# Routed expert tiles: transposes between the two projections, TensorE in written order, gathers three tiles ahead

## The chip, the core and the metric

The kernel runs on one core of a Trainium2 chip. The core has five engines with a queue each: TensorE (PE in the profile; PEld is its weight load), VectorE (DVE), ScalarE (ACT), GpSimd (POOL) and SyncE (SP), and 16 DMA engines that move data between memory and the on-chip buffers. Instructions of one engine run in the order of its queue; engines wait for one another by semaphores. The metric is the device time of one execution in microseconds (us), and lower is better.

## What is computed

The reference is one decoder layer over 4 sequences of 512 tokens with 512 features, all in float32: a causal self-attention, a cross-attention against a context, and a feed-forward part, each behind a layer norm and added to its input. Only the last part matters here. Each token is sent to 2 of 8 experts; each expert is a gated network with 352 hidden units.

```python
topk_p, topk_i = jax.lax.top_k(probs, K)                 # K = 2 of E = 8 experts
comb = (jax.nn.one_hot(topk_i, E) * topk_p[..., None]).sum(axis=1)
h1 = jnp.einsum('nc,eic->eni', xf, w1)                   # 512 -> 352, for each expert
h2 = jnp.einsum('nc,eic->eni', xf, w2)
h = jax.nn.silu(h1) * h2
eo = jnp.einsum('eni,eci->enc', h, w3)                   # 352 -> 512
y = jnp.einsum('enc,ne->nc', eo, comb).reshape(Bq, Tq, Cq)
sh = jax.nn.silu(xf @ sw1.T) * (xf @ sw2.T) @ sw3.T      # shared expert, every token
return y + sh.reshape(Bq, Tq, Cq)
```

## The kernel before

The two attentions, the shared expert and the choice of experts fill the first 1729 us and are the same in both kernels. At their end `out` holds the result without the routed part, and `normed` (in memory) holds the normed tokens.

**Routing.** The kernel computes only what the router asks for. The 4096 pairs of a token and an expert are sorted by expert and cut into tiles of 128 rows, each of one expert, with padding: `NTILE` = 39 tiles. `picked[:, t]` holds the token numbers of tile t, `gain[:, t]` the weights, `owner[0, t]` the expert. Which expert a tile has is known only at run time, so PE reads it into a register (L1088, a TENSOR_LOAD in the profile) and addresses `w1all`, `w2all` and `w3all`, which hold the weights of all experts, by it. For the same reason a wait for these weights covers the loads of all experts.

**One tile, first half: `enter`.** `fetch` (L1050) gathers 128 rows into `xg` by an indirect DMA on POOL's queue (L1053; four buffers), PE turns them in four transposes (L171, by `transpose_in`) into a bank of PSUM, and ScalarE copies the bank to `xT` (L172). Then come PE's read of the owner, the projections h1 and h2 (L1102: for each four matmuls over 352 columns, which the profile shows as eight), the silu of h1 on ScalarE (L1110, `sl`), and the product `hm` on VectorE (L1112).

**Second half: `leave`.** PE turns `hm` in three transposes into `ht` (L1118; one bank), VectorE copies it to `hT` in two pieces (L1120, L1121), PE multiplies it with w3 into `y` (L1124; three matmuls over 512 columns, six in the profile; one bank), ScalarE scales it into `yo` (L1132; two buffers), and POOL issues an indirect DMA (L1134) that adds the rows to `out`. These scatter-adds all write `out`, so each waits for the one before.

**Order.** The loop (L1146) enters tile t and then leaves tile t - 4 (`BEHIND` = 4); four tiles are left after the loop. The program is written in that order, but the framework's scheduler decides the order of the instructions on each engine, except where `tc.keep_in_program_order` is called on an instruction. Here only the owner's read is held. In the steady part the scheduler makes it, on PE: h1, h2 of tile t; ht of tile t - 4; the transposes of the rows of tile t + 1; the owner of tile t + 1; y of tile t - 4. On VectorE it is hm, then the two hT copies; on POOL gathers and scatters alternate. The class `Ordered` (L356) wraps an engine so that its instructions are held in program order while `pinned` is true; `tensor` is PE wrapped so. The attention part uses it and sets `pinned` back to False at L896. The wrapper's line, L362, is then the line that the profile shows.

**Before the loop.** The first two tiles' rows are fetched among the last jobs of the shared expert (L1068). The loads of w3 (L1081, L1084) are on SP's queue and start when the shared expert's weights are no longer needed, at 1728.3 us. The loads of w1 and w2 (L1047, L1048) are issued before that, the last at 1681.0 us.

Of the kernel before, what the change touches and what calls it, by code (L numbers as in the profile page):

```python
# [8 lines left out]
F32 = mybir.dt.float32  # L9
BF16 = mybir.dt.bfloat16  # L10
AF = mybir.ActivationFunctionType
ALU = mybir.AluOpType
# [3 lines left out]
P = 128  # L16
B, S, HID = 4, 512, 512
NT = S // P
NC = HID // P
NKV, QPG, D = 4, 4, 128  # L20
XKV, XG, XD = 8, 4, 16
E, I = 8, 352
# [5 lines left out]
NTILE = (2 * B * S + E * (P - 1)) // P  # L28
# [7 lines left out]
def decoder_kernel(  # L36
# [15 lines left out]
    nc = tc.nc  # L52
# [5 lines left out]
    ident = const.tile([P, P], F32, tag="ident", name="ident")  # L58
# [108 lines left out]
    def transpose_in(ps, src, dst, s, copy, bufs=2):  # L167

        t = ps.tile([P, NC, P], F32, tag="t", name="t", bufs=bufs)
        for c in range(NC):  # L170
            nc.tensor.transpose(t[:, c, :], src[:, c * P : (c + 1) * P], ident)  # L171
        copy(dst[:, :, s * P : (s + 1) * P], t)  # L172
# [6 lines left out]
    with ExitStack() as ph:  # L179
        wp = ph.enter_context(tc.tile_pool(name="wattn", bufs=1))  # L180
        p2 = ph.enter_context(tc.tile_pool(name="a2", bufs=2))
        ps = ph.enter_context(tc.tile_pool(name="aps", bufs=2, space=PSUM))
# [7 lines left out]
        for g in range(NKV):  # L190
            t = wp.tile([P, NC, (QPG + 1) * D], F32, tag=f"wqk{g}", name=f"wqk{g}")
            nc.sync.dma_start(t, wqkv_v[:, :, g, : (QPG + 1) * D])
            wqk.append(t)
            t = pj.tile([P, QPG, HID], F32, tag=f"wpr{g}", name=f"wpr{g}")
# [37 lines left out]
        def project(b, g, h, xnT):  # L232

            pq = ps.tile([P, S], F32, tag="mm", name=f"pq{b}_{g}_{h}")
            for c in range(NC):
                nc.tensor.matmul(  # L236
                    pq,
                    lhsT=wqk[g][:, c, h * D : (h + 1) * D],
                    rhs=xnT[:, c, :],
                    start=c == 0,  # L240
                    stop=c == NC - 1,
                )
            if h == QPG:
                t = p2.tile([P, S], F32, tag="kT", name=f"kT{b}_{g}")
                nc.scalar.copy(t, pq)
            else:
                t = p2.tile([P, S], F32, tag="qT", name=f"qT{b}_{g}_{h}", bufs=3)
                nc.scalar.mul(t, pq, QSCALE)  # L248
            return t
# [71 lines left out]
        late = None  # L321
# [10 lines left out]
        for b in range(B):  # L332
            xnT, v = norm_and_v(b)
            for g in range(NKV):
                kT = project(b, g, QPG, xnT)
                outs = []
                for h in range(QPG):
# [4 lines left out]
                    late = (b, g, h, pr, v, outs)  # L342
# [11 lines left out]
    pinned = False  # L354

    class Ordered:  # L356
# [12 lines left out]
    tensor, vector, scalar, gpsimd, sync = (  # L369
        Ordered(e) for e in (nc.tensor, nc.vector, nc.scalar, nc.gpsimd, nc.sync)  # L370
    )
# [108 lines left out]
    with ExitStack() as ph:  # L480
# [45 lines left out]
        def enter(b):  # L526

            xn = p2.tile([P, NT, HID], F32, tag="xn", name=f"cxn{b}", bufs=1)
            parts = norm_parts(
                b, lambda s: xn[:, s, :], vector, gpsimd, vector if b == 0 else gpsimd  # L530
            )
            ctxT = p2.tile([P, S], F32, tag="ctxT", name=f"ctxT{b}", bufs=1)
            xnT = p2.tile([P, NC, S], F32, tag="xnT", name=f"cxnT{b}", bufs=1)
            ctxTs[b], xnTs[b] = ctxT, xnT

            def values():
                gpsimd.tensor_copy(
                    vpad[b % 2][:, :, :, 0:XD],
                    ctxs[b].rearrange("p s (k d) -> p s k d", d=XD),
                )  # L540

            def keys():
                t = single(f"tc{b}")
                for s in range(NT):
                    tensor.transpose(quarter(t, s), ctxs[b][:, s, :], ident)
                scalar.copy(ctxT, t)

            def tokens(s):
                t = single(f"tx{b}_{s}")
                for c in range(NC):  # L550
                    tensor.transpose(quarter(t, c), xn[:, s, c * P : (c + 1) * P], ident)
                scalar.copy(
                    xnT[:, :, s * P : (s + 1) * P],
                    t.rearrange("p (c d) -> p c d", c=NC),
                )

            return parts + [values], [keys] + [lambda s=s: tokens(s) for s in range(NT)]
# [245 lines left out]
        pinned = True  # L803
# [6 lines left out]
        for i in range(NU * 8 + LAG + 4):  # L810
# [35 lines left out]
            b, u = divmod(n, XKV)  # L846
# [57 lines left out]
    with ExitStack() as ph:  # L904
# [142 lines left out]
            nc.sync.dma_start(w1all[:, e], w1T[e].rearrange("(c p) i -> p c i", p=P))  # L1047
            nc.sync.dma_start(w2all[:, e], w2T[e].rearrange("(c p) i -> p c i", p=P))  # L1048

        def fetch(t, ps, bufs):  # L1050

            xg = rx.tile([P, HID], F32, tag="xg", name=f"xg{t}", bufs=4)
            nc.gpsimd.indirect_dma_start(  # L1053
                out=xg,
                out_offset=None,
                in_=normed,
                in_offset=bass.IndirectOffsetOnAxis(ap=picked[:, t : t + 1], axis=0),
            )
            xT = rx.tile([P, NC, P], F32, tag="xT", name=f"xT{t}")
            transpose_in(ps, xg, xT, 0, nc.scalar.copy, bufs)  # L1060
            return xT

        jobs = shared_jobs(
            B - 1, lambda name: ps.tile([P, S], F32, tag="fill", name=name, bufs=4)
        )
        for job in jobs[:-12]:
            job()
        fetched = [fetch(t, ps, 1) for t in range(2)]  # L1068
        for job in jobs[-12:]:
            job()  # L1070
    late_sh.close()
# [3 lines left out]
    with ExitStack() as ph:  # L1075
        wl = ph.enter_context(tc.tile_pool(name="wall3", bufs=1, side="right"))
        p2 = ph.enter_context(tc.tile_pool(name="r2", bufs=2))
        ps = ph.enter_context(tc.tile_pool(name="rps", bufs=2, space=PSUM))
        w3all = wl.tile([P, E, len(IC), HID], F32, tag="w3all", name="w3all")
        for e in range(E):  # L1080
            nc.sync.dma_start(  # L1081
                w3all[:, e, 0:2, :], w3T[e, 0:256].rearrange("(c p) d -> p c d", p=P)
            )
            nc.sync.dma_start(w3all[0 : I - 256, e, 2, :], w3T[e, 256:I])  # L1084

        def enter(t):
            xT = fetched[t] if t < len(fetched) else fetch(t, ps, 2)
            loads, (e,) = nc.values_load_multi_w_load_instructions(  # L1088
                owner[0:1, t : t + 1],
                engines=[mybir.EngineType.PE],  # L1090
                min_val=0,
                max_val=E - 1,
                skip_runtime_bounds_check_because="a count of at most E - 1 by its minimum",
                bass_reorder=False,
            )
            for i in loads:
                tc.keep_in_program_order(i)
            h1 = ps.tile([P, I], F32, tag="h1", name=f"h1_{t}")
            h2 = ps.tile([P, I], F32, tag="h2", name=f"h2_{t}")
            for h, w in ((h1, w1all), (h2, w2all)):  # L1100
                for c in range(NC):
                    nc.tensor.matmul(  # L1102
                        h,
                        lhsT=xT[:, c, :],
                        rhs=w[:, e, c, :],
                        start=c == 0,
                        stop=c == NC - 1,
                    )
            sl = p2.tile([P, I], F32, tag="sl", name=f"sl{t}")
            nc.scalar.activation(sl, h1, AF.Silu)  # L1110
            hm = p2.tile([P, I], F32, tag="hm", name=f"hm{t}", bufs=BEHIND + 2)
            nc.vector.tensor_tensor(hm, h2, sl, ALU.mult)  # L1112
            return t, e, hm

        def leave(t, e, hm):
            ht = ps.tile([P, len(IC), P], F32, tag="ht", name=f"ht{t}", bufs=1)
            for ic, (i0, m) in enumerate(IC):
                nc.tensor.transpose(ht[:m, ic, :], hm[:, i0 : i0 + m], ident)  # L1118
            hT = p2.tile([P, len(IC), P], F32, tag="hT", name=f"hT{t}")
            nc.vector.tensor_copy(hT[:, 0:2, :], ht[:, 0:2, :])  # L1120
            nc.vector.tensor_copy(hT[: I - 256, 2, :], ht[: I - 256, 2, :])  # L1121
            y = ps.tile([P, HID], F32, tag="y", name=f"y{t}", bufs=1)
            for ic, (_, m) in enumerate(IC):
                nc.tensor.matmul(  # L1124
                    y,
                    lhsT=hT[:m, ic, :],
                    rhs=w3all[:m, e, ic, :],
                    start=ic == 0,
                    stop=ic == len(IC) - 1,
                )  # L1130
            yo = p2.tile([P, HID], F32, tag="yo", name=f"yo{t}", bufs=2)
            nc.scalar.activation(yo, y, AF.Copy, scale=gain[:, t : t + 1])  # L1132

            nc.gpsimd.indirect_dma_start(  # L1134
                out=rows,
                out_offset=bass.IndirectOffsetOnAxis(ap=picked[:, t : t + 1], axis=0),
                in_=yo,
                in_offset=None,
                bounds_check=B * S - 1,
                oob_is_err=False,  # L1140
                compute_op=ALU.add,
            )

        BEHIND = 4
        late = []
        for t in range(NTILE):  # L1146
            late.append(enter(t))
            if len(late) > BEHIND:
                leave(*late.pop(0))
        for now in late:  # L1150
            leave(*now)


# [46 lines left out]
```

## Time and profile before

| | |
|---|---|
| median of 3 runs | 2084.8 us (2084.55 to 2087.17) |
| the profiled execution | 2085.54 us |
| its span, first to last instruction | 2083.8 us |
| TensorE clock granted, mean | 0.997 |
| PE busy over the span | 2029.6 us (97%) |
| VectorE, ScalarE, POOL busy over the span | 864.6, 679.5, 197.3 us |

The routed part in stages, from the profile's windows (us from the span's start; busy time of each engine):

| stage | length | PE | VectorE | ScalarE | POOL | DMA share |
|---|---|---|---|---|---|---|
| 1729.2 to 1757.9: tiles entered before the first is left | 28.7 | 26.91 | 3.02 | 5.75 | 3.04 | 0.82 |
| 1905.1 to 2043.7: the steady loop, 16 tiles of it | 138.6 | 133.04 | 16.78 | 27.77 | 38.03 | 0.28 |
| 2043.7 to 2070.2: the last y of the steady loop, and the tail | 26.5 | 23.26 | 3.55 | 4.22 | 6.20 | 0.24 |
| 2070.2 to 2083.8: after the last matmul | 13.6 | 0 | 0 | 0.69 | 3.10 | 0.01 |

A row of the timeline reads: start, length, engine, line, operation, output and input, how many; in square brackets the idle time of the engine just before it and what ended it. Matmuls are pipelined, so the length of one is longer than its share of PE: the distance from one start to the next is what it costs. "128x352" is partitions by elements. An entry that ends in q, like PEldq, is the engine's sequencer, which runs control instructions and does not count as busy.

### The profile page before, as it was taken

What the parts mean: (1) busy time and instruction counts of PE and PEld (TensorE: products, weight loads), DVE (VectorE), ACT (ScalarE), POOL (GpSimd) and SP (SyncE); (2) the same over time, 40 slices, a digit from 0 to 9 for tenths busy, and PEclk for the clock granted to TensorE, in tenths of its full rate; (3) what the DMA queues carried; (4) which work ended last, traced back from release to release, by engine and by line L of the source; (5) the groups of instructions that cost most, each with busy time, mean ns of one, the idle gap of its engine ahead of it and who ended that gap; (6) DMA issues with size and microseconds to landing.
All of it is one profiled execution on the core that took longest, in us unless ns stands there. A gap on an engine that the chain in (4) does not pass through costs nothing. (4 is left out here: it accounts for less than half of the span.)

```text
span 2083.8 us, 22685 instructions
## 1 busy us (share of the span) xinstructions
PE 2029.6 (97%) x8507; PEld 948.5 (46%) x8507; DVE 864.6 (41%) x1843; ACT 679.5 (33%) x1479; POOL 197.3 (9%) x182
## 2 busy tenths in 40 slices
PE   7999999999999999999999999999999999999996
PEld 4555555554555555542233333333333445555553
DVE  4433344442344334436666656566563351111111
ACT  2322332232223323323555454444444101111121
POOL 1000000000000000010202202020200011222222
PEclk9999999999999999999999999999999999999999
DMA  7000000000000000010003100100110255323321
GB/s 282 0 1 0 1 0 1 0 0 1 0 1 0 1 0 0 1 32 14 16 16 100 32 16 22 42 15 13 42 27 1 95 199 160 59 56 57 57 49 23
DMA packets 52509, 74.81 MB, mean 36 GB/s; under 512 B 9889, under 2 KB 27809, under 8 KB 52402
## 3 DMA queue, kind: packets, MB, share of 16 engines
q1 hardware_dynamic: 43666, 54.73, 8.5%
q0 software_dynamic: 8736, 18.62, 4.7%
q8 instruction: 70, 1.15, 0.2%
q14 instruction: 37, 0.30, 0.0%
HBM read 47.60 MB, written 18.61 MB: 32 GB/s over the span
## 5 line engine op out<-in xcount | busy, mean ns | idle before, releaser
L362 DVE TENSOR_REDUCE cnmx<-s 128x1 f32<-128x512 f32 x512 | 329.3, 685 | 199.3 <-PE s L362 199.2
L362 ACT ACTIVATE w<-s 128x512 f32<-128x512 f32 x512 | 277.9, 595 | 339.0 <-PE s L362 338.9
L362 PE MATMUL s<-ckT,cqT 32*128 32x512 f32 x1024 | 308.8, 640 | 1.0 <-DVE cnmx L362 1.0
L236 PE MATMUL pq<-xnT,wqk 128*128 128x512 f32 x640 | 300.9, 593 | 0.0
L362 PE MATMUL s<-cqT,ckT 32*128 32x512 f32 x1024 | 294.8, 640 | 0.0
L268 DVE TENSOR_REDUCE nmx<-sc 128x1 f32<-128x128 f32 (+3 forms) x256 | 125.8, 491 | 185.0 <-PE sc L265 184.8
L271 ACT ACTIVATE pr<-sc,nmx 128x128 f32<-128x128 f32 (+3 forms) x256 | 135.0, 527 | 156.0 <-DVE nmx L268 156.0
L294 DVE COPY prT<-tp 128x128 f32<-128x128 f32 (+2 forms) x192 | 97.0, 507 | 206.4 <-PE tp L290 206.3
L258 PE MATMUL sc<-kT,qT 128*128 128x128 f32 (+3 forms) x512 | 181.4, 463 | 0.0
L312 PE MATMUL pj<-wpr,oT 128*128 128x512 f32 x384 | 171.8, 596 | 0.0
L362 PE MATMUL sh<-fnT,sw 128*128 128x512 f32 x320 | 154.0, 613 | 0.0
L297 PE MATMUL po<-prT,v 128*128 128x512 f32 (+3 forms) x512 | 149.5, 434 | 4.3 <-DVE prT L294 4.3
L236 PEld LDWEIGHTS pq<-xnT,wqk 128*128 128x128 f32 x640 | 110.7, 191 | 85.5 <-issue 85.4
L362 PEld LDWEIGHTS s<-cqT,ckT 32*128 32x128 f32 x1024 | 80.7, 183 | 145.3 <-ACT w L362 108.6
L1112 DVE TENSOR_TENSOR hm<-h,sl 128x352 f32<-128x352 f32 x39 | 20.5, 525 | 284.6 <-PE h L1102 279.1
L362 PE MATMUL cpo<-w,vpad 128*32 128x512 f32 x1024 | 137.3, 608 | 0.0
L297 PEld LDWEIGHTS po<-prT,v 128*128 128x128 f32 x512 | 96.8, 190 | 84.3 <-issue 45.4
L1124 PE MATMUL y<-w3all,hT 128*128 (+1 forms) x234 | 109.8, 605 | 15.1 <-DVE hT L1120 15.1
L248 ACT ACTIVATE qT<-pq 128x512 f32<-128x512 f32 x64 | 38.2, 597 | 225.0 <-PE pq L236 225.0
L258 PEld LDWEIGHTS sc<-kT,qT 128*128 128x128 f32 x512 | 81.6, 189 | 56.1 <-ACT qT L248 20.2
L312 PEld LDWEIGHTS pj<-wpr,oT 128*128 128x128 f32 x384 | 69.5, 190 | 77.3 <-issue 71.0
L290 PE MATMUL tp<-ident,pr 128*128 128x128 f32 x640 | 102.3, 275 | 1.3 <-DVE prT L294 1.3
(162 smaller groups left out, 2000.6 us busy)
## 6 DMA issues: line engine op xcount, KB each, us to landing
w1all<-in_w1T SPq DMA_DIRECT2D x8, 704.0 KB
w2all<-in_w2T SPq DMA_DIRECT2D x8, 704.0 KB
wqk<-in_wqkvT SPq DMA_DIRECT2D x4, 1280.0 KB
x<-in_x SPq DMA_DIRECT2D x4, 1024.0 KB
wpr<-in_wprojT SPq DMA_DIRECT2D x4, 1024.0 KB
cqT<-cxnT SPq DMA_DIRECT2D x128, 32.0 KB
ckT<-ctxT SPq DMA_DIRECT2D x128, 32.0 KB
normed<-fxn SPq DMA_DIRECT2D x4, 1024.0 KB
```

Source lines behind the costliest of these rows:

```text
L236: nc.tensor.matmul(pq, lhsT=wqk[g][:, c, h * D : (h + 1) * D], rhs=xnT[:, c, :], start=c == 0, stop=c == NC - 1,)
L248: nc.scalar.mul(t, pq, QSCALE)
L258: nc.tensor.matmul(sc[:, :n], lhsT=qT[:, i * P : n], rhs=kT[:, :n], start=True, stop=False,)
L268: nc.vector.tensor_reduce(nmx[:, i : i + 1], sc[:, :n], AX.X, ALU.max, negate=True)
L271: nc.scalar.activation(pr[:, OFF[i] : OFF[i] + n], sc[:, :n], AF.Exp, bias=nmx[:, i : i + 1], accum_out=sm[:, i : i + 1],)
L290: nc.tensor.transpose(t[:, j, :], pr[:, OFF[i] + j * P : OFF[i] + (j + 1) * P], ident)
L294: copy(prT[:, : i + 1, i * P : (i + 1) * P], t[:, : i + 1, :])
L297: nc.tensor.matmul(po[:, j * P :], lhsT=v[j][:, g, :], rhs=prT[:, j, j * P :], start=j == 0, stop=j == NT - 1,)
L312: nc.tensor.matmul(pj, lhsT=outs[h][:, s * P : (s + 1) * P], rhs=wpr[g][:, h, :], start=h == 0, stop=h == QPG - 1,)
L362: i = getattr(self.engine, name)(*args, **kw)
L1112: nc.vector.tensor_tensor(hm, h2, sl, ALU.mult)
L1124: nc.tensor.matmul(y, lhsT=hT[:m, ic, :], rhs=w3all[:m, e, ic, :], start=ic == 0, stop=ic == len(IC) - 1,)
```

## The change

`fetch` is split: `gather_rows(t)` issues the gather, `turn_rows(t)` the four transposes and the copy to `xT`. Gathers of three tiles are issued before the loop, and each pass of the loop begins with that of tile t + 3; `xg` still has four buffers. `enter` and `leave` are split too. One pass of the loop is now, in this order: the gather of t + 3, the owner of tile t, h1 and its silu; the ht transposes and hT copies of the oldest waiting tile; the transposes of the rows of tile t + 1; h2 and hm; and last y, yo and the scatter of the waiting tile. All PE instructions of the loop go through `tensor` with `pinned` true, so this is their order on PE. How many tiles are left in a pass is `count`: none in tiles 0 to 3, one from tile 4 on, and two in tiles 12, 16 and 20, after which a tile is left one pass after it was entered, and one tile is left after the loop. The second of two does its ht transposes after h2. Banks and buffers keep their numbers. On PE the owner's read stands between y of one pass and h1 of the next; on VectorE the hT copies stand before hm. SP's queue keeps its order.

```diff
-        def fetch(t, ps, bufs):
-
+        xgs, xTs = {}, {}
+
+        def gather_rows(t):
             xg = rx.tile([P, HID], F32, tag="xg", name=f"xg{t}", bufs=4)
             nc.gpsimd.indirect_dma_start(
...
+            xgs[t] = xg
+
+        def turn_rows(t, ps, bufs=2):
+
             xT = rx.tile([P, NC, P], F32, tag="xT", name=f"xT{t}")
-            transpose_in(ps, xg, xT, 0, nc.scalar.copy, bufs)
-            return xT
+            bank = ps.tile([P, NC, P], F32, tag="t", name=f"xt{t}", bufs=bufs)
+            for c in range(NC):
+                tensor.transpose(bank[:, c, :], xgs[t][:, c * P : (c + 1) * P], ident)
+            nc.scalar.copy(xT, bank)
+            xTs[t] = xT
...
-        fetched = [fetch(t, ps, 1) for t in range(2)]
+        for t in range(3):
+            gather_rows(t)
+        for t in range(2):
+            turn_rows(t, ps, 1)
...
-        def enter(t):
-            xT = fetched[t] if t < len(fetched) else fetch(t, ps, 2)
+        def owner_of(t):
             loads, (e,) = nc.values_load_multi_w_load_instructions(
...
+            return e
+
+        def project(t, e, w, tag):
+            h = ps.tile([P, I], F32, tag=tag, name=f"{tag}_{t}")
+            for c in range(NC):
+                tensor.matmul(
+                    h,
+                    lhsT=xTs[t][:, c, :],
...
+            return h
+
+        def turn_hidden(t, hm):
             ht = ps.tile([P, len(IC), P], F32, tag="ht", name=f"ht{t}", bufs=1)
             for ic, (i0, m) in enumerate(IC):
-                nc.tensor.transpose(ht[:m, ic, :], hm[:, i0 : i0 + m], ident)
+                tensor.transpose(ht[:m, ic, :], hm[:, i0 : i0 + m], ident)
             hT = p2.tile([P, len(IC), P], F32, tag="hT", name=f"hT{t}")
             nc.vector.tensor_copy(hT[:, 0:2, :], ht[:, 0:2, :])
             nc.vector.tensor_copy(hT[: I - 256, 2, :], ht[: I - 256, 2, :])
+            return hT
+
+        def leave(t, e, hT):
...
         BEHIND = 4
+        pinned = True
         late = []
         for t in range(NTILE):
-            late.append(enter(t))
-            if len(late) > BEHIND:
-                leave(*late.pop(0))
-        for now in late:
-            leave(*now)
+            if t + 3 < NTILE:
+                gather_rows(t + 3)
+            e = owner_of(t)
+            h1 = project(t, e, w1all, "h1")
+            sl = p2.tile([P, I], F32, tag="sl", name=f"sl{t}")
+            nc.scalar.activation(sl, h1, AF.Silu)
+            count = 0 if t < BEHIND else 2 if len(late) > 1 and t % 4 == 0 and t > 8 else 1
+            now, late = late[:count], late[count:]
+            turned = [(u, o, turn_hidden(u, hm)) for u, o, hm in now[:1]]
+            if 1 < t + 1 < NTILE:
+                turn_rows(t + 1, ps)
+            h2 = project(t, e, w2all, "h2")
+            hm = p2.tile([P, I], F32, tag="hm", name=f"hm{t}", bufs=BEHIND + 2)
+            nc.vector.tensor_tensor(hm, h2, sl, ALU.mult)
+            late.append((t, e, hm))
+            turned += [(u, o, turn_hidden(u, hm)) for u, o, hm in now[1:]]
+            for some in turned:
+                leave(*some)
+        for u, o, hm in late:
+            leave(u, o, turn_hidden(u, hm))
+        pinned = False
```

More of the change, by code (lines that the diff above doesn't have):

```diff
@@ L1097, in enter @@
                 tc.keep_in_program_order(i)
[L1098 to L1115, printed above, removed]
+            return e
[5 more added lines that the diff above has]
+                    lhsT=xTs[t][:, c, :],
+                    rhs=w[:, e, c, :],
+                    start=c == 0,
+                    stop=c == NC - 1,
+                )
+            return h
+        def turn_hidden(t, hm):
             ht = ps.tile([P, len(IC), P], F32, tag="ht", name=f"ht{t}", bufs=1)
             for ic, (i0, m) in enumerate(IC):
-                nc.tensor.transpose(ht[:m, ic, :], hm[:, i0 : i0 + m], ident)
+                tensor.transpose(ht[:m, ic, :], hm[:, i0 : i0 + m], ident)
             hT = p2.tile([P, len(IC), P], F32, tag="hT", name=f"hT{t}")
@@ L1121, in leave @@
             nc.vector.tensor_copy(hT[: I - 256, 2, :], ht[: I - 256, 2, :])
+            return hT
+        def leave(t, e, hT):
             y = ps.tile([P, HID], F32, tag="y", name=f"y{t}", bufs=1)
             for ic, (_, m) in enumerate(IC):
-                nc.tensor.matmul(
+                tensor.matmul(
                     y,
@@ L1130, in leave @@
                 )
-            yo = p2.tile([P, HID], F32, tag="yo", name=f"yo{t}", bufs=2)
+            yo = p2.tile([P, HID], F32, tag="yo", name=f"yo{t}")
             nc.scalar.activation(yo, y, AF.Copy, scale=gain[:, t : t + 1])
```

## The prediction

> **What bounds the kernel now.** I read the page first (TensorE, PE in the rows, is busy 97% of the span), then the PE timeline of the routed tiles, where all of the diff lies, then the rows of all engines around one wait there, then the tail. PE's timeline, one tile of the steady part and the start of the next (start, length, operation, idle time before):
>
> ```profile
> 1847.17 2.53 PE L1102 MATMUL h<-w1all,xT 128*128 x8
> 1849.54 2.53 PE L1102 MATMUL h<-w2all,xT 128*128 x8
> 1851.91 0.49 PE L1118 MATMUL ht<-ident,hm 128*128 128x128 f32 x3
> 1852.24 0.60 PE L171 MATMUL t<-ident,xg 128*128 128x128 f32 x4
> 1853.18 2.82 PE L1124 MATMUL y<-w3all,hT 128*128 x6 [0.34 <-DVE hT L1120]
> 1855.83 2.53 PE L1102 MATMUL h<-w1all,xT 128*128 x8
> ```
>
> A tile takes 8.66 us (1847.17 to 1855.83). PE's own work is, start to start: both projections 2 x 2.37, three ht transposes 0.33, four t transposes 4 x 0.11 (three starts in 0.60 less one length of 0.27), y 6 x 0.43 = 2.57: 8.08. Lost are **0.58 us a tile**: 0.50 between the t transposes and y, and 0.08 because y's first weight load then stands open (2.65 from y to the next h instead of 2.57). The rows around the wait say why:
>
> ```profile
> 1912.52 0.49 PE L1118 MATMUL ht<-ident,hm 128*128 128x128 f32 x3
> ...
> 1912.79 0.53 DVE L1112 TENSOR_TENSOR hm<-h,sl 128x352 f32<-128x352 f32 x1 [7.61 <-PE h L1102]
> 1912.85 0.60 PE L171 MATMUL t<-ident,xg 128*128 128x128 f32 x4
> 1913.23 0.41 DVE L1120 COPY hT<-ht 128x256 f32<-128x256 f32 x1
> ...
> 1913.57 0.28 DVE L1121 COPY hT<-ht 96x128 f32<-96x128 f32 x1
> ...
> 1913.80 2.82 PE L1124 MATMUL y<-w3all,hT 128*128 x6 [0.35 <-DVE hT L1120]
> ```
>
> y needs hT, hT waits on VectorE behind hm, and hm could only start when h2 ended. Only 0.44 us of transposes cover that. Nothing else is near: in 1905.14:2043.70 the granted clock is 1.00 and the DMA share 0.28. The end of the kernel:
>
> ```profile
> 2063.61 2.82 PE L1124 MATMUL y<-w3all,hT 128*128 x6 [0.61 <-DVE hT L1120]
> ...
> 2066.99 1.55 POOL L1134 DMA_INDIRECT out<-yo,picked  x1 [3.88 <-issue]
> ...
> 2067.36 2.82 PE L1124 MATMUL y<-w3all,hT 128*128 x6 [0.61 <-DVE hT L1120]
> ...
> 2070.63 0.69 ACT L1132 ACTIVATE yo<-y,gain 128x512 f32<-128x512 f32 x1 [3.44 <-DMA out<-yo,picked]
> 2071.28 1.55 POOL L1134 DMA_INDIRECT out<-yo,picked  x1 [2.73 <-DMA out<-yo,picked]
> 2074.72 1.55 POOL L1134 DMA_INDIRECT out<-yo,picked  x1 [1.90 <-DMA out<-yo,picked]
> ```
>
> Four second halves are left after the loop. Each y comes 3.75 us after the last (2063.61 to 2067.36) against 2.90 of work, and the scatter-adds, which follow one another (starts 5.36, 5.42, 4.29 and 3.44 us apart), are by then the last to finish: from the last y to the end of the span 16.44 us.
>
> **The change, part by part.** Work on PE up to the start of the last y is the same in both: 78 projections x 2.37 + 37 sets of t x 0.44 (two stand before the loop) + 39 ht x 0.33 + 38 y x 2.57 = 311.8 us. Before, it took 2067.36 - 1729.21 = 338.2: 26.4 us lost, namely 34 tiles x 0.58 = 19.7; 1.0 at the y of tile 34; four tail leaves x 0.85 = 3.4; tiles 2 to 4, whose h1 waits for its own xT, 1.6; the rest is rounding.
>
> - *Both sets of transposes between h1 and h2.* The hT copies now run beside h2. In the tail, where no hm is in front of them, y can start 1.10 us after the first ht (2066.26 to 2067.36); in the change ht, t and h2 last 0.33 + 0.44 + 2.37 = 3.14: 2.0 us to spare. hm falls behind them on VectorE and is next needed a tile later. xT (0.58 on ScalarE) hides behind the same h2. So the 0.58 goes in all 35 steady leaves, and the 1.6 of tiles 2 to 4. What is late next is PE itself; ScalarE's order stays silu, xT, yo.
> - *A new border, transposes to a projection, 37 times.* The nearest row is before the loop, four t transposes and then a matmul of the shared part: 1717.61 to 1718.08, 0.47 against 0.44 of work, and 0.49 the time before. I take 0.04 each: 1.5 us. Bounds: 0, and one open weight load of 0.19 (mean of h's loads), 7 us.
> - *The read of the tile's owner* (L1088) stood between t and y, beside the wait; now it stands between y and h1, where no stall covers it:
>
> ```profile
> L1088 PEldq TENSOR_LOAD <-owner x39: 295/301/826, 1720.3 to 2039.2; - x39
> ```
>
>   Median 0.30 us. Behind it on PE's queue are h1 and all that follows. The last one ran at 2039.2, while the transposes it follows end at about 2043.3: the sequencer is 4 us ahead. In the change it is held at y's wait until hT is there, some 2 us before y can start, and y runs 2.57 more. Tile 1 already has the new order (h2, read, h1) and no gap: the next rows show h2 at 1731.65 and h1 at 1734.02, 2.37 apart. Here a rule speaks against the change: the Trainium skill ("DMA: Bandwidth & Descriptors", Latency and other measured facts) gives a tensor_load a floor of about 600 ns. Exposed in 35 tiles that is 21 us, an estimate, and nearly all of the gain; by the row 35 x 0.30 = 10.5. The row decides the size, tile 1 the cover: I take 0 and keep 10.5 as the bound.
>
> ```profile
> 1729.21 2.61 PE L1102 MATMUL h<-w1all,xT 128*128 x8 [0.94 <-issue]
> 1731.65 2.53 PE L1102 MATMUL h<-w2all,xT 128*128 x8
> 1734.02 2.53 PE L1102 MATMUL h<-w1all,xT 128*128 x8
> ```
>
> - *Gathers three tiles ahead:* nothing. There are four buffers as before; POOL already issues four gathers at 1689.6 to 1693.7 and the fifth at 1717.19 when tile 0 is transposed. One lands in 3.4 us (8.2 at worst), needed two tiles later. On POOL's queue a gather can stand behind a scatter; it has 16 us to spare. SP's list is unchanged.
> - *Two leaves in tiles 12, 16 and 20.* y has one bank, so the second waits for yo of the first: as in the tail 3.75 against 2.57, 1.18 each, 3.5 us. Their scatters go out 3.75 apart, and the next 8 us later: no queue builds up.
> - *w3.* Any y waits for all of w3, because the expert is a number known at run time. y of tile 0 comes at 1729.21 + 4.74 + 3 x 5.22 + 5.55 = 1755.2 instead of 1757.89. The DMA windows:
>
> ```profile
> 1752.00:1754.00 2.00, 2.00 (x7) 1.31 (x8) 0.00 (x0) 0.00 (x0) 0.36 (x1) 1.00 0.44 137
> 1754.00:1756.00 2.00, 2.00 (x8) 1.32 (x7) 0.00 (x0) 0.46 (x1) 0.00 (x0) 1.00 0.04 14
> ```
>
>   The load (last two numbers: DMA share, GB/s) ends by about 1754: I take 0, bound 1.5.
> - *The tail.* One leave is left; its y waits for hm, ht and yo as each tail y did: 0.85.
>
> Lost after: 1.5 + 3.5 + 0.85 = 5.9, so the last y starts at 1729.2 + 311.8 + 5.9 = 2046.9, 20.4 us earlier. From there: 2.90 to yo (1913.80 to 1916.70), 0.96 to the scatter, 9.08 from its start to the end (2074.72 to 2083.8), and 0.55 because the scatter before it was issued 3.75 ago and I take 4.3 between two (bounds 0 and 1.7): 13.5 instead of 16.4. Span 2060.4, **23.4 us less**. The profiled execution took 2085.54 (1.74 over its span): 2062.1. The median of the runs stands 0.74 lower: **2061.4**.
>
> **The rivals.**
> - *A rest of the stall stays at the new borders* (the owner's read exposed by its 0.30, or an open weight load at each): +7 to +10.5, 2068 to 2072. For it: y's wait still holds PE's sequencer once a tile. Against: 2 us of cover, and tile 1.
> - *The period stays at 8.66,* so that the change does not do what it says, because something other than hT ends the wait. Then the tail (3.4 - 0.85 + 2.9), less 3.5 for the double leaves, plus 1.6 at the start: 3.6 us less, 2081. Against: 0.16 us lies between the first hT copy's end (1913.64) and y, every tile.
> - *PE drains at the owner's read (slower).* Tile 0 shows the price: between the shared part's last matmul and h1 lie 0.94 us, put down to "issue", with the read waiting for semaphores. If y's wait leaves the queue empty in each of 35 tiles: 2061.4 + 32.9 = 2094. It decides from 23.4 / 35 = 0.67 us a tile. Against: tile 0's read waits for PE itself, the others do not.
>
> **How the numbers follow.** Forecast 0.78, rest of the stall 0.12, period unchanged 0.05, drain 0.05. Low end: no border cost, no scatter wait, and some 2 us for rows that I read as full: 2056. High end: the first rival's 2072. That leaves out the last two, 0.10, and a little. This kernel's measurement can tell 0.2%, 4.2 us, from no change: faster 0.90; the unchanged period, at 3.6, counts as the same: 0.05; slower 0.05.
>
> **What would show it.** In the changed kernel: a period near 8.1 us wherever one tile is left; no idle row before y except in tiles 12, 16, 20 and the last; h2 0.77 to 0.85 after the first ht; h1 2.57 after y's start; last y near 2047; 13 to 14 us from it to the end. A wait before h1 put down to "issue" would make the first or third rival right, an idle row before y the second, a DMA wait at tile 0's y the w3 term.

## The result and the profile after

The changed kernel takes **2060.86 us** (median of 4 runs, 2059.55 to 2061.09); the kernel before, run beside it, 2085.94 (4 runs, 2084.55 to 2087.17). The ratio is 0.9879, with a 95% interval of 0.9862 to 0.9896: some 25 us less. The profiled execution after took 2059.55 us, with a span of 2057.7 and a granted clock of 0.998. The first projection of tile 0 (h1) starts at 1729.31 us, against 1729.21 before, so all of the difference lies in the routed tiles.

TensorE's timeline after, a steady tile with the start of the next, and then the two adjacent y in the pass of tile 12 (columns as before; line 362 is the helper that now issues every TensorE instruction):

```profile
1757.71 2.53 PE L362 MATMUL h<-w1all,xT 128*128 x8
1760.08 0.49 PE L362 MATMUL ht<-ident,hm 128*128 128x128 f32 x3
1760.40 0.60 PE L362 MATMUL xt<-ident,xg 128*128 128x128 f32 x4
1760.84 2.53 PE L362 MATMUL h<-w2all,xT 128*128 x8
1763.21 2.74 PE L362 MATMUL y<-w3all,hT 128*128 x6
1765.79 2.53 PE L362 MATMUL h<-w1all,xT 128*128 x8
...
1820.09 2.74 PE L362 MATMUL y<-w3all,hT 128*128 x6
1823.66 2.84 PE L362 MATMUL y<-w3all,hT 128*128 x6 [0.83 <-ACT yo L1142]
```

A tile takes 8.08 us (1757.71 to 1765.79), and no row in it has idle time in brackets. The transposes take 0.76 us from the first start to h2, as much as their work. Where two tiles are left, the second y starts 3.57 us after the first instead of 2.57, because it waits for ScalarE to empty the one y bank.

The same stretch of work on all engines, later in the loop, shows why y no longer waits:

```profile
1909.95 0.42 DVE L1127 COPY hT<-ht 128x256 f32<-128x256 f32 x1 [4.68 <-PE ht L362]
...
1910.29 0.28 DVE L1128 COPY hT<-ht 96x128 f32<-96x128 f32 x1
...
1912.55 2.74 PE L362 MATMUL y<-w3all,hT 128*128 x6
...
1912.82 0.52 DVE L1174 TENSOR_TENSOR hm<-h,sl 128x352 f32<-128x352 f32 x1 [2.26 <-PE h L362]
```

hT is complete at 1910.57, two microseconds before y starts. VectorE then sits idle 2.26 us for h2, and hm, which stood in front of hT before, comes behind it and beside y.

In the cost table by line, the idle time before y fell from 15.1 us to 3.1: 2.5 for yo in the three double leaves and 0.6 for hT in the last. In the end of the span, only that last y stalls:

```profile
2043.95 0.49 PE L362 MATMUL ht<-ident,hm 128*128 128x128 f32 x3
...
2045.05 2.81 PE L362 MATMUL y<-w3all,hT 128*128 x6 [0.61 <-DVE hT L1127]
2045.16 1.55 POOL L1144 DMA_INDIRECT out<-yo,picked  x1 [6.09 <-ACT yo L1142]
...
2048.91 1.55 POOL L1144 DMA_INDIRECT out<-yo,picked  x1 [2.20 <-ACT yo L1142]
```

The last y starts 22.3 us earlier than before, and from there to the end it takes 12.65 us, not 16.44. The bracket of the last scatter names yo, not a DMA: nothing is queued in front of it.

### The profile page after: what moved, and what is told of

It is laid out like the page before. It is cut to its first block, busy times and chain, and to the rows that moved or that the text cites. A ratio compares the mean times of both kernels' runs of the same rounds, so it can differ in the third digit from the quotient of the medians.

```text
span 2057.7 us, 22666 instructions
## 1 busy us (share of the span) xinstructions
PE 2020.7 (98%) x8507; PEld 946.0 (46%) x8507; DVE 867.4 (42%) x1843; ACT 680.0 (33%) x1479; POOL 197.8 (10%) x182
## 5 line engine op out<-in xcount | busy, mean ns | idle before, releaser
L290 PEld LDWEIGHTS tp<-ident,pr 128*128 128x128 f32 x640 | 71.9, 141 | 62.6 <-issue 43.6
```

Source lines behind the costliest of these rows:

```text
L290: nc.tensor.transpose(t[:, j, :], pr[:, OFF[i] + j * P : OFF[i] + (j + 1) * P], ident)
```

## The experiments

The first part of the kernel, which nobody touched, took between 1726.62 and 1730.56 us in these profiles. So the runs are compared by their **routed stage**, from the start of the first h1 to the end of the span: 354.6 us before, **328.4** after. Times of whole runs stand beside it. Runs of the kernel before made next to the experiments had medians of 2086.16 and 2086.75 us (7 runs each); two later single ones took 2087.6 and 2085.19. The mean granted clock of every profiled execution was 0.997 to 0.999.

The theory: y starts late because hT is late, and what cures it is that the ht transposes have h2 behind them. The rivals: the two orders of transposes act separately; the gain comes from holding TensorE in written order, from the earlier gathers, or from the shorter tail; and the owner's read is a hidden cost. A "..." in an edit or in rows marks what is left out.

### Both sets of transposes back behind h2

```diff
-            turned = [(u, o, turn_hidden(u, hm)) for u, o, hm in now[:1]]
-            if 1 < t + 1 < NTILE:
-                turn_rows(t + 1, ps)
             h2 = project(t, e, w2all, "h2")
...
             late.append((t, e, hm))
+            turned = [(u, o, turn_hidden(u, hm)) for u, o, hm in now[:1]]
+            if 1 < t + 1 < NTILE:
+                turn_rows(t + 1, ps)
```

> Both sets of transposes are put back behind h2, all else of the change is kept (order held, gathers three ahead, double leaves, one tile left at the end). Theory A (the gain is the hT copies' cover): the stall before y is back, period 8.66 instead of 8.08 in 35 tiles, +20, and tiles 2 to 4 wait for their xT again, +2: near 2083 us. Rival B (the held order or the earlier gathers bring the gain): stays near 2061. Rival C (the shorter tail brings most of it): about 2065.

2083.01 us in a single execution, with a routed stage of 352.9: **24.5 us of the 26.2 are gone**. The period is 8.66 again, with 0.35 us of idle time for hT ahead of y. Written order, gathers, double leaves and short tail are all still in this kernel; together they are worth 1.7 us. A tile on TensorE's timeline of this kernel:

```profile
1889.71 2.53 PE L362 MATMUL h<-w1all,xT 128*128 x8
1892.07 2.53 PE L362 MATMUL h<-w2all,xT 128*128 x8
1894.44 0.49 PE L362 MATMUL ht<-ident,hm 128*128 128x128 f32 x3
1894.77 0.60 PE L362 MATMUL xt<-ident,xg 128*128 128x128 f32 x4
1895.71 2.81 PE L362 MATMUL y<-w3all,hT 128*128 x6 [0.35 <-DVE hT L1127]
1898.37 2.53 PE L362 MATMUL h<-w1all,xT 128*128 x8
```

### One set of transposes between the projections

Only the four xt (the next tile's rows) stay in between; ht goes back behind h2:

```diff
-            turned = [(u, o, turn_hidden(u, hm)) for u, o, hm in now[:1]]
             if 1 < t + 1 < NTILE:
                 turn_rows(t + 1, ps)
...
             late.append((t, e, hm))
+            turned = [(u, o, turn_hidden(u, hm)) for u, o, hm in now[:1]]
```

> Only the rows' transposes (xT) stay between h1 and h2; ht stands behind h2, directly ahead of y. Theory A: nothing lies beside the hT copies any more, y starts 1.28 after the first ht (0.95 of stall and 0.08 for the open weight load): period 9.1, +36 us, near 2097, slower than before the change. Rival D (it is xT's place that gains): near 2061.

2094.53 us in a single execution, routed stage 364.9: 10.3 us **slower** than the kernel before. TensorE's timeline of this kernel:

```profile
1895.67 2.53 PE L362 MATMUL h<-w2all,xT 128*128 x8
1898.04 0.49 PE L362 MATMUL ht<-ident,hm 128*128 128x128 f32 x3
1899.32 2.81 PE L362 MATMUL y<-w3all,hT 128*128 x6 [0.78 <-DVE hT L1127]
```

From ht to y it takes 1.28 us, as it did before (1851.91 to 1853.18, 1.27). That distance belongs to hm and the two copies on VectorE. In the kernel before, the xt transposes filled 0.44 us of it; here they have left, nothing has come in, and the idle time before y is 0.78.

The reverse, only ht in between and xt behind h2:

```diff
             turned = [(u, o, turn_hidden(u, hm)) for u, o, hm in now[:1]]
-            if 1 < t + 1 < NTILE:
-                turn_rows(t + 1, ps)
             h2 = project(t, e, w2all, "h2")
...
             late.append((t, e, hm))
+            if 1 < t + 1 < NTILE:
+                turn_rows(t + 1, ps)
```

> Only ht stays between h1 and h2; the rows' transposes stand behind h2, ahead of y. Theory A: xT's copy is covered by y's 2.57, so the period stays 8.08; only tiles 2 to 4, which have no y ahead of them, wait 0.7 each: +2, near 2063 us. Rival D (xT's place gains): near 2081.

2061.15 us, ratio to before 0.9884 (0.9867 to 0.9900), routed stage 331.35: 3.0 us more than the changed kernel. Nearly all of it (2.9 us, by the start of tile 0's y) lies in tiles 2 to 4, which have no y yet to stand between xt and h1. One of them on TensorE's timeline of this kernel:

```profile
1737.49 0.60 PE L362 MATMUL xt<-ident,xg 128*128 128x128 f32 x4
1738.77 2.63 PE L362 MATMUL h<-w1all,xT 128*128 x8 [0.68 <-ACT xT L1068]
```

So **ht between the projections is worth 21.6 us** (352.9 to 331.35). xt between them adds 3.0 if ht is there too, and costs 12.0 (352.9 to 364.9) if it isn't: the parts don't add up separately.

The move does two things to the wait: h2 now covers the copies, and the copies no longer stand behind hm. No run tried the second alone, but the tails give an estimate of it. There no hm is in front, and y starts 1.10 us after the first ht (2043.95 to 2045.05 in the changed kernel) instead of 1.27. That is 0.17 of the 0.50 us of idle time; the other 0.33 would have stayed.

### The kernel before, held in its written order

The order of instructions is not touched in the text; TensorE only keeps to it (the transposes and y go through `tensor` in the same way):

```diff
...
-                    nc.tensor.matmul(
+                    tensor.matmul(
...
         BEHIND = 4
+        pinned = True
...
```

> The kernel before with nothing changed but that TensorE's instructions of the routed loop are held in program order (transposes of a tile's rows directly ahead of its h1, ht directly ahead of y). Theory A: a held order is worth only what its places cover; here it uncovers both copies: xT 0.62 + 0.07 and hT 0.95 + 0.08 a tile, period 9.8 instead of 8.66: +39, near 2125 us. Rival B (holding the order is itself a gain): at or under 2085.

2137.46 us in a single execution, routed stage 406.5, **51.9 us longer** than before, where I expected 39. The period is 10.17 us, not 9.8. The rows of all engines show what I missed:

```profile
1893.38 0.69 ACT L1135 ACTIVATE yo<-y,gain 128x512 f32<-128x512 f32 x1 [5.82 <-PE y L362]
1893.97 0.58 ACT L1063 COPY xT<-xt 128x512 f32<-128x512 f32 x1
...
1894.60 2.63 PE L362 MATMUL h<-w1all,xT 128*128 x8 [0.86 <-ACT xT L1063]
```

In the written order xt follows y directly. So xT queues on ScalarE behind yo, and h1 starts 1.47 us after xt (1893.13 to 1894.60) with 0.86 us idle. The scheduler had moved the transposes ahead of y. Holding the order is not what makes the change fast: it makes the text's order count, good or bad.

The changed kernel, with its order left to the scheduler:

```diff
         BEHIND = 4
-        pinned = True
         late = []
```

> The change's program, with the order on TensorE left to the scheduler. On TensorE it differs only in tiles 12, 16 and 20, where the next tile's ht and rows' transposes come ahead of the second y. Theory A: the held order is worth nothing; 0.77 of the 1.0 us that the second y waits is filled three times: -2.3, near 2058.5 us. Rival B (holding the order gains): slower than 2061 by several us.

**2056.29 us** (2055.83 to 2057.26), ratio 0.9860 (0.9843 to 0.9876); routed stage 326.1, 2.3 us less than the changed kernel, as expected. TensorE's timeline of the first double leave:

```profile
1818.66 2.74 PE L362 MATMUL y<-w3all,hT 128*128 x6
1821.24 0.49 PE L362 MATMUL ht<-ident,hm 128*128 128x128 f32 x3
1821.57 0.60 PE L362 MATMUL xt<-ident,xg 128*128 128x128 f32 x4
1822.23 2.85 PE L362 MATMUL y<-w3all,hT 128*128 x6
```

While ScalarE empties the y bank, the scheduler runs the transposes of the next pass, which need nothing of it. The second y still starts 3.57 us after the first, but 0.76 us of that is now work.

### The second half: one behind, and a second bank

Leaving one tile at a time, four behind to the end as before:

```diff
-            count = 0 if t < BEHIND else 2 if len(late) > 1 and t % 4 == 0 and t > 8 else 1
+            count = 0 if t < BEHIND else 1
```

> The change with one leave a tile all through: no double leaves, four tiles left after the loop as before. Theory A: the three waits for yo go, -3.0; three more tail leaves at 0.85 over their work, +2.5, and the scatters queue at the end again, from the last y to the end 16.4 instead of 12.65, +3.8: near 2064 us. Rival C (catching up is most of the gain): over 2075.

2061.64 us (2061.31 to 2062.00), ratio 0.9884 (0.9868 to 0.9901); routed stage 331.8, 3.4 us more than the changed kernel. The end of it on POOL and ScalarE:

```profile
2046.42 0.69 ACT L1142 ACTIVATE yo<-y,gain 128x512 f32<-128x512 f32 x1 [3.67 <-DMA out<-yo,picked]
2047.07 1.55 POOL L1144 DMA_INDIRECT out<-yo,picked  x1 [2.82 <-DMA out<-yo,picked]
2050.51 1.55 POOL L1144 DMA_INDIRECT out<-yo,picked  x1 [1.90 <-DMA out<-yo,picked]
```

The last y comes 315.0 us after the first h1, which is 0.7 *earlier* than in the changed kernel: three double leaves cost 0.7 us more than three leaves in the tail. But after it the end takes 16.8 us, not 12.65. The brackets shown here name a DMA: the scatter-adds queue behind one another (2037.07, 2042.70, 2047.07, 2050.51; that of 2042.70 is put down to "issue"). What the double leaves bring is that their scatters are gone in time.

The double leaves without their wait: the second y of a double, and the last y of all, go to a bank that the transposes leave free, and the last ht stands ahead of the third part of the y before it:

```diff
-        def leave(t, e, hT):
-            y = ps.tile([P, HID], F32, tag="y", name=f"y{t}", bufs=1)
+        def leave(t, e, hT, second=False, amid=None):
+            if second:
+                y = ps.tile([P, NC, P], F32, tag="t", name=f"y{t}", bufs=2)
+                y = y.rearrange("p c d -> p (c d)")
+            else:
+                y = ps.tile([P, HID], F32, tag="y", name=f"y{t}", bufs=1)
             for ic, (_, m) in enumerate(IC):
+                if amid is not None and ic == len(IC) - 1:
+                    amid()
...
```

> The change, but the second y of a double leave and the very last y go into the free bank of the rows' transposes, and the last ht stands ahead of the third part of the y before it. Theory A: the wait for yo goes, -3.0, and the last y comes 2.90 after the one before instead of 3.68, of which the last scatter may give back up to 0.8: near 2057 us. Rival (the wait was covered elsewhere): 2061.

**2056.49 us** (2055.43 to 2057.65), ratio 0.9858 (0.9841 to 0.9874); routed stage 325.1, 3.3 us less than the changed kernel and the shortest of all. A double leave on its TensorE timeline is one piece of work:

```profile
1821.34 5.32 PE L362 MATMUL y<-w3all,hT 128*128 x12
1826.50 2.53 PE L362 MATMUL h<-w1all,xT 128*128 x8
```

No y waits any more. The end then meets the next bound: the last scatter-add, issued 3.45 us after the one before it (2043.46 to 2046.91), waits for that one's transfer.

### The gathers

The distance at which the gathers are written, two tiles and one instead of three. This is the edit for two; for one it is `gather_rows(t + 1)`. Both write two gathers ahead of the loop instead of three:

```diff
...
-            if t + 3 < NTILE:
-                gather_rows(t + 3)
+            if t + 2 < NTILE:
+                gather_rows(t + 2)
```

> The change with gathers two tiles ahead instead of three. Theory A: a gather then goes out about 3 us after h1's start behind the scatter on POOL's queue, lands 3.4 us later, and is needed more than one tile after that: no change, 2061 us within the runs' 2 us. Rival (the depth of three pays): a DMA wait ahead of the rows' transposes, over 2070.

> The change with gathers one tile ahead. Theory A: on POOL's queue the gather stands behind the scatter, which starts 1.2 after h1 and takes 1.6; so it starts near 3.0, lands near 6.4, and the rows' transposes are due 2.7 after h1's start: a stall of 3.7 us a tile, +137, near 2198 us. This is the price of the depth if it is missing. Rival (the gather passes the scatter): a stall of about 1 us, near 2095.

2056.87 and 2060.69 us in a single execution each, with routed stages of 328.4 and 328.5: the same as the change. The 137 us that one theory expected of the distance of one did not come, which does not show that such a distance is harmless. The order of POOL's instructions is the same in both as in the changed kernel: four gathers ahead of the loop, and then one for each buffer that comes free. The kernel before also starts with four, so this part of the change moved nothing. The scheduler hoists each gather to where its buffer comes free: in the changed kernel one is issued at 1910.62, held last by the xt transposes of 1909.74, which empty that buffer. The two runs say only that the written distance does not reach the queue.

What does limit the distance is the number of buffers:

```diff
-            xg = rx.tile([P, HID], F32, tag="xg", name=f"xg{t}", bufs=4)
+            xg = rx.tile([P, HID], F32, tag="xg", name=f"xg{t}", bufs=2)
```

> The change with two buffers for gathered rows instead of four, so that a gather can be at most two tiles ahead whatever the written distance. Theory A: a gather then goes out when the rows two tiles before it have been transposed, 3.1 us into a tile, lands 4 us later (9.0 at worst, while w3 loads) and is needed 8 us after it went out (10 in the first tiles): no DMA wait ahead of the rows' transposes, from the first h1 to the end 328.4 us as in the change, at most 1 us more. Rival (depth pays): waits for the gather ahead of the rows' transposes, 340 us or more from the first h1 to the end.

2057.77 us in a single execution, routed stage 328.45, no wait for a gather before any xt. A gather lands in 3.9 us at the median and 8.4 at worst, and with two buffers there are still two tiles, 16 us, between the transposes that free a buffer and those that read it again. Fetching far ahead is worth nothing here.

### The read of the owner

Four reads of the tile's owner, or eight, instead of one, ahead of h1; each matmul takes its own (the edit for eight):

```diff
-                    rhs=w[:, e, c, :],
+                    rhs=w[:, e[c], c, :],
...
-            e = owner_of(t)
-            h1 = project(t, e, w1all, "h1")
+            es = [owner_of(t) for _ in range(8)]
+            e = es[0]
+            h1 = project(t, es[:4], w1all, "h1")
...
-            h2 = project(t, e, w2all, "h2")
+            h2 = project(t, es[-4:], w2all, "h2")
```

> The owner is read four times a tile instead of once, all four ahead of h1, each read used by one part of h1. The read started 4.3 us ahead of h1 and took 0.73. Theory A (the read is covered because the sequencer runs ahead): 2.9 us of reads, still covered, 2061 us. Rival E (TensorE drains at a read, the forecast's slower rival in a milder form): 2.2 us more a tile, near 2140.

> Eight reads a tile ahead of h1, used by the parts of h1 and h2. Theory A: at 0.73 each they take 5.8 us, more than the 4.3 of cover: a stall of 1.5 to 1.8 us a tile ahead of h1, near 2120 us; at 0.30 each, as the reads took before the change, 2.4 us and no stall, 2061. Rival E: 5 us more a tile, near 2250.

With four: 2058.41 us in a single execution, routed stage 328.4, the same as with one. With eight: 2063.44 us, routed stage 333.4, 5.0 more, some 4.3 of it behind the three double leaves (h1 comes 4.24, 4.25 and 3.90 us after the second y instead of 2.68). The last of these on the TensorE timeline with eight reads:

```profile
1898.86 2.85 PE L362 MATMUL y<-w3all,hT 128*128 x6 [0.83 <-ACT yo L1142]
1902.76 2.63 PE L362 MATMUL h<-w1all,xT 128*128 x8 [1.06 <-issue]
```

There the second y, which waits for yo, holds the sequencer until it starts. The eight reads run from 1899.1 to 1902.5, past 1901.54, where h1 would stand, and h1 follows the last by 0.26 us. In a normal tile the sequencer is let go when hT is there: the eight reads of one run from 1914.7 to 1918.3 (y at 1916.43), and h1 follows at 1919.01 with no idle row, so eight just fit. The single read of the changed kernel has the least cover behind a double leave, too: the last of these reads starts at 1896.6 and takes 0.30 us, and h1 stands at 1898.97. By the same 0.26 us from read to h1, some 1.9 us are to spare.

## Why the prediction was right

The forecast was 2061.4 us; it came to 2060.86. Its case, no stall left in a steady tile, is the one that happened. By its steps:

- **The 0.58 us a tile.** Right: 8.66 to 8.08, and h2 0.76 us after the first ht. Putting both orders of transposes back returned 24.5 of 26.2 us. The experiments sharpen the reason: ht behind h2 is the cause (21.6 us), xt a small addition.
- **The new border, 1.5 us.** Over-sized: measured 0. From xt to h2 it takes 0.44 us, which is its work.
- **The owner's read, 0, bound 10.5.** The 0 was right, and so was its reason. The row I sized it by was not: at the median a read after the change takes longer than both my row of 0.30 and the rule of about 600 ns from the Trainium skill ("DMA: Bandwidth & Descriptors", Latency and other measured facts). That rule is given as a floor, and as a floor it does not hold here, with reads of 0.296:

```profile
L1098 PEldq TENSOR_LOAD <-owner x39: 296/726/859, 1720.3 to 2032.0; - x39
```

  The median of 39 is 0.726 us. Had it been exposed in 35 tiles it would have cost 25 us, nearly all of the gain. But around the rows above the read runs at 1910.8 and h1 starts at 1915.13: 4.3 us ahead. The cover decided, not the size; reads four times over changed nothing.
- **Gathers, 0.** Right, with two buffers as well.
- **Double leaves, 3.5 us.** 3.3: the second y starts 1.0 us late (3.57 against 2.57), and h1 follows it after 2.68 instead of 2.58. The size was near, but the reason was another. I took the tail's 3.75 between two y as the wait for yo. The tail's rows put that wait down to hT, because there ht follows the y before it; here ht stands ahead of both, and the second y does wait for yo.
- **w3, 0.** Right: y of tile 0 starts at 1755.13, where 1755.2 was worked out, without a wait.
- **The tail.** One leave at 0.85 was 0.78 (3.68 from y to y, less 2.57 and 0.33). From the last y to the end it was 12.65 instead of 13.5: the 0.55 for a scatter that waits was not needed at 3.75 us between two, and the rest, 0.3, is the last transfer and what follows, 8.8 instead of 9.08 us.

The work itself was right to 0.2 us: from the first h1 to the last y 315.74, less 3.3 and 0.78, leaves 311.7 against 311.8. The four small terms (border 1.5, doubles 0.2, tail 0.07, end 0.85) were together 2.6 us too large, so the span came to 2057.7 instead of 2060.4. The median of the runs hides that: the profiled execution was the quickest of its kernel, 1.3 us under the median, while I had taken one that is 0.74 over it. That the forecast stands only 0.5 us from the median is luck: two misses of more than 2 us cancel. The period and the cover of the read are not luck: both were read off rows and came out so.

The rivals. *A rest of the stall at the borders:* not there, neither as an idle row nor in the period. *The period stays:* fell at once. *PE drains at the read:* no wait before h1 except at tile 0, and with eight reads it appears only where y itself was held until its start. A slower outcome was nearer than I had it, though by another way: with only xt moved, or with a written order in which xT stands behind yo, kernels with the same TensorE work lose 10 and 52 us.

## What to carry to other kernels

When an engine waits for a chain on other engines that it started itself (transpose, copy, product), put a long independent piece of its own work between the start of the chain and its use, and measure the chain from its first instruction to its last to see whether the piece is long enough (here 1.27 us against 2.37 of h2). Work that is moved out of a stall must be replaced there: moving only xt made the kernel slower. A cost on a sequencer is read from how far ahead that sequencer is at that place, not from the duration of the instruction; and of the versions run here, the scheduler's order (2056.29 us) and the second bank (2056.49 us) have lower medians than the change. They were not run beside the change; by routed stage they are 2.3 and 3.3 us shorter.

## What the runs showed of the hardware that I had not expected

- The same read of one number into a register took 0.30 us at the median before and 0.73 after. It is not simply that y now stands ahead of it: of the 34 reads behind a y in the changed kernel, eight took 0.36 us or less, among them the three behind double leaves. With eight in a row in a steady tile, the first took 0.75 us and the others 0.30, one every 0.40 us; behind the last double leave the first took 0.30 and the sixth 0.61. The cause stays open.
- The untouched part of 1729 us varies by almost 4 us from run to run: with POOL's order the same, the first h1 started at 1726.62 in one execution and at 1730.44 in the other, while the routed stages agreed to 0.1 us. The granted clock from 1600 to 1700 us was 0.97 in the two profiles whose first h1 is latest (1730.44 and 1730.56) and 1.00 in the other twelve, which still lie 2.7 us apart. So the clock can be a part of it and not the whole; the cause was not shown. Effects of 2 to 3 us can be seen in the stage and hardly in the whole time: the intervals of the whole-time ratios of the three quickest versions overlap.
- A scatter-add follows the one before it at 3.4 to 5.6 us when they queue, and at 3.75 us without any wait for it in the changed kernel. So whether it waits can't be told from the distance alone. The row's bracket says more, though two that queue (2066.99 before, 2042.70 with four behind) are put down to "issue".
